# A graph layer on one core: self-edges taken out of the edge stream and added once per node block, packed rows stored end to end, one unit in 75 fetched row by row by SyncE

## The chip, the cores and the metric

The kernel runs on one core of one Trainium2 chip. The metric is the device time of one execution in microseconds, lower is better; the profile is one further execution of the same program with the hardware profiler on.

## The reference

There are 50,000 nodes with 160 numbers each (64 scalars `s`, then 32 vectors of 3) and 1,650,000 edges: 800,000 random pairs in both directions and one self-edge per node. The edges are sorted by their destination, so a node has 33 of them on average, one of which starts at the node itself. Every edge carries 4 numbers `sh`, and its message is bilinear in the source's row and these four:

```python
ss, vv = s[src], v[src];  e0, e1 = sh[:, 0:1], sh[:, 1:4]
dot  = einsum('eui,ei->eu', vv, e1)
out0 = C0 * (ss * e0 @ W1 + dot * INV3 @ W2)
p3 = (ss @ W3)[:, :, None] * e1[:, None, :] * INV3
p4 = einsum('eui,uw->ewi', vv * e0[:, :, None], W4) * INV3
p5 = einsum('eui,uw->ewi', cross(vv, e1[:, None, :]), W5) * INV6
m  = concat([out0, (C1 * (p3 + p4 + p5)).reshape(-1, 96)], axis=1)
m_agg = segment_sum(m, dst, num_segments=n)
h  = concat([m_agg[:, :64] @ Ws * LIN_S, (m_agg's vectors @ Wv) * LIN_V], axis=1)
x  = layernorm(x + (x + relu(h)))
```

All of it is linear in the source's row up to the relu. So for each node one may first sum, over its edges, the source's row times each of the four edge numbers (4 x 160 sums per node), and multiply that by one combined matrix of 640 x 160 afterwards. For a self-edge the source's row is the node's own, so its message needs no gathered row at all.

## The kernel before

*Units, groups, pairs, chunks, blocks.* 128 edges are a unit; 6 units (`G`) are a group of 768 edges, whose destinations lie in a window of 32 nodes (`W`); 2 groups are a pair, the step of the main loop (L637); 4 groups are a chunk of 128 window rows (`QG`); 20 groups, so 10 pairs, are a super group (`SG`), the amount that one load of edges brings. There are 1,050 pairs and 525 chunks. Output nodes are taken in 391 blocks of 128 (the last is shorter).

*One pair.* `gather` (L288) has GpSimd issue one indirect DMA per unit (L292), which brings the 128 source rows of 640 bytes into `xg`, on 6 buffers. `spread` (L297) has VectorE build, from each edge's place in the window (`rel`) and its four numbers (`pk`), a matrix `ha` of 128 edges x 128 columns (4 numbers x 32 window nodes) for each of 12 units (L301, L304), one pair ahead. `group_sums` (L329) has TensorE add up `ha` transposed times `xg`, 6 products per group (L334), into `ps` (128 x 160 per group, two groups a buffer). `ps` is then moved to `A` on 4 buffers, as the next paragraphs say.

*After a chunk.* At fixed numbers of pairs later (`after_pair`, L591, L662 to L669) the chunk is transposed (`turn`, L459), multiplied by the combined weights (`apply_weights`, L476, giving `hp`), and, once the last chunk that touches a node block is there, `nodes` loads the block's rows `xt` and builds one-hot matrices of the window rows' nodes (L493), `block` sums the rows `hp` of three chunks or so into nodes (L512), and the norm and the store of `out` follow over three more pairs.

*Loading edges.* `load` (L235) brings one super group's sources, destinations and numbers a super group ahead, `cast` makes floats of them, and `place` (L267) transposes them, so that each edge of a unit has a partition, and writes the gather indices `si` (L277) and `rel`. The destination of every group's first edge is read once at the start, out of DRAM into DRAM by three DMAs (L559, 2,020 numbers for the packed part) and back, broadcast to all partitions (L561), as `baseB`.

*Packing.* The first 60 groups (`NH`) are taken as they are. Each later group is made from a row of 786 edges (`L`), of which up to 18 (`K`) self-edges are taken out so that 768 remain. `pack` (L354) does this for 120 rows (`RP`), a row on each partition, 17 times in all: it reads the rows (`pri`, `pra`), marks self-edges and counts them (L390 to L398), collects the four numbers of each self-edge by window node into `mine` (L415 to L423, L419 most of all), moves the remaining edges down in 5 shifts of 1, 2, 4, 8, 16 places (L431 to L448), and stores 120 groups of 768 with three DMAs (L454, L455) into DRAM, from where `load` takes them. `pack` is a generator; the main loop advances it evenly over the 60 pairs until its rows are needed (L654 to L661), the first one over the 20 pairs or so that the head gives.

*The taken self-edges.* For each packed pair `own` (L311) loads the rows of x of both windows, repeated 4 times, into `xo` (one DMA per group, L324, at an address that is read from a table into a register, ten at a time, L318). When the pair's sums are done, VectorE moves `ps` to `A` and adds `xo` times the collected numbers `taken` (L343); for the head groups ScalarE copies (L339).

*Who issues what.* All these DMAs stand on SyncE's one queue (`dq`, L231), the gathers on GpSimd's, and seven loads of weights and three more on ScalarE's. `HELP` (L63) is empty: `fetch` (L537), which would load some units row by row from SyncE or ScalarE, one DMA per row at an address from a register, issues nothing. The order on each engine is that in which the program text emits instructions, as changed by the scheduler of the build; the buffers of the pools and semaphores do the rest. After the main loop a second pass over the edges stands in the program, with a loop count of zero unless a check on the data (L688) fails; both kernels have it alike.

Here is how one pair's gathers stand to the helped units, of which there are none in this kernel:

```python
for j in range(n - len(others)):
    nc.gpsimd.indirect_dma_start(out=xg[:, j, :], ..., in_=x, ...)
return [xg[:, j, :] for j in range(n - len(others))] + others
```

Of the kernel before, what the change touches and what calls it, by code (L numbers as in the profile page):

```python
# [25 lines left out]

# [17 lines left out]
P = 128  # L45
MUL0, MUL1 = 64, 32
D = MUL0 + 3 * MUL1
NK = 4
# [14 lines left out]
HELP = {}  # L63
HEAD = 60
RP = 120

# [3 lines left out]
def plan(n_nodes, n_edges):  # L70

    nblk = 125
    assert n_nodes % nblk == 0
    nb = n_nodes // nblk
    again = 9

    per_unit = P * n_nodes / n_edges
    group = max(g for g in range(1, 17)
                if g == 1 or (g + 0.2) * per_unit + 1 + 5 * math.sqrt(g * per_unit * per_unit / P) <= W)

    out = 0
    while out + 1 <= per_unit * group * (1 + 0.03) - 5 * math.sqrt(group * per_unit * per_unit / P + 1 / 6):
        out += 1
    row = group * P + out
    head = min(HEAD, math.ceil(n_edges / (group * P)))
    packed = max(0, (n_edges - head * group * P) // row // SG * SG) if out else 0
    rest = max(0, n_edges - head * group * P - packed * row)
    ngroups = head + packed + math.ceil(rest / (group * P))
    padded = QG * math.ceil(ngroups / QG)
    end = (head + padded - head - packed) * group * P + packed * row  # L90
    units = P * math.ceil(max(math.ceil(n_edges / P) + again - 1, math.ceil(end / P)) / P)
    return nblk, nb, again, group, units, ngroups, row, head, packed
# [3 lines left out]
def tile_gnn_resnorm(ctx: ExitStack, tc: tile.TileContext, x, src, dst, attr, W1, W2, W3, W4, W5, Ws, Wv, out, n_edges):  # L96
    nc = tc.nc
    N = x.shape[0]
    NBLK, NB, GA, G, NU, NG, L, NH, NPK = plan(N, n_edges)
    NCH = math.ceil(NG / QG)  # L100
    NGP = NCH * QG
    K = L - G * P

    def start(g):

        packed = min(max(g - NH, 0), NPK)
        return (g - packed) * G * P + packed * L

# [88 lines left out]
    def near(c):  # L197
        return start(c * QG) * N / n_edges

    step = QG * max(G * P, L) * N / n_edges  # L200
    off = 6 * math.sqrt(n_edges) / 2 * N / n_edges + W
# [10 lines left out]
    with tc.tile_pool(name="once", bufs=1) as once, tc.tile_pool(name="raw", bufs=2) as rawp, \  # L212
            tc.tile_pool(name="idx", bufs=2) as idxp, tc.tile_pool(name="rows", bufs=6) as rowp, \
            tc.tile_pool(name="far", bufs=3) as farp, tc.tile_pool(name="own", bufs=5) as ownp, \
            tc.tile_pool(name="pack", bufs=1) as packp, tc.tile_pool(name="self", bufs=2) as selfp, \
            tc.tile_pool(name="ops", bufs=3) as op, tc.tile_pool(name="sums", bufs=4) as sump, \
# [3 lines left out]
            tc.tile_pool(name="psM", bufs=2, space=PSUM) as psM:  # L220

        extremes = once.tile([P, 2, NSC], F32, name="extremes")
        baseB = once.tile([P, NGP], F32, name="baseB")
        rowid = once.tile([P, NCH], F32, name="rowid")
        bank = psC.tile([P, 3, P], F32, name="bank")
# [3 lines left out]

        own_eng = ET.Activation if ET.SP in HELP else ET.SP  # L230
        dq = nc.scalar if ET.SP in HELP else nc.sync  # L231
# [3 lines left out]
        def load(s):  # L235

            n = (min(NG, (s + 1) * SG) - s * SG) * G
            g0 = s * SG
            ra = rawp.tile([P, P, NK], F32, name="ra")
            if NH <= g0 < NH + NPK:  # L240
                sd, ad = stored[(g0 - NH) // RP]
                e = slice((g0 - NH) % RP * G * P, ((g0 - NH) % RP * G + n) * P)
                rf = rawp.tile([P, 2, P], F32, name="rf")
                for i in range(2):
                    dq.dma_start(rf[:n, i, :], sd[i:i + 1, e].rearrange("o (u p) -> (o u) p", p=P))
                dq.dma_start(ra[:n].rearrange("u p k -> u (p k)"), ad[e].rearrange("(u p) k -> u (p k)", p=P))
                return s, n, None, rf, ra
            e = slice(start(g0), start(g0) + n * P)
            ri = rawp.tile([P, 2, P], I32, name="ri")
            dq.dma_start(ri[:n, 0, :], src1[e].rearrange("(u p) o -> u (p o)", p=P))  # L250
            dq.dma_start(ri[:n, 1, :], dst1[e].rearrange("(u p) o -> u (p o)", p=P))
            dq.dma_start(ra[:n].rearrange("u p k -> u (p k)"), attr[e].rearrange("(u p) k -> u (p k)", p=P))
            return s, n, ri, None, ra

        def cast(loaded):
            s, n, ri, rf, ra = loaded
            if rf is None:
                rf = rawp.tile([P, 2, P], F32, name="rf")
                nc.scalar.copy(rf[:n], ri[:n])
            if HELP:  # L260

                ro = rawp.tile([P, P], I32, name="ro")
                nc.scalar.mul(ro[:n], rf[:n, 0, :], 4.0 * D)
                offsets[s] = ro
            return s, n, rf, ra

        def place(cast_):  # L267

            s, n, rf, ra = cast_
            pi = bank[:, 1:3, :]  # L270
            for i in range(2):
                nc.tensor.transpose(pi[:, i, :n], rf[:n, i, :], ident[:n, :n])
            pk = psK.tile([P, NK, P], F32, name="pk")
            for k in range(NK):
                nc.tensor.transpose(pk[:, k, :n], ra[:n, :, k], ident[:n, :n])
            si = idxp.tile([P, P], I32, name="si")
            nc.vector.tensor_copy(si[:, :n], pi[:, 0, :n])  # L277
# [4 lines left out]
                float(N - 1), baseB[:, s * SG:s * SG + n // G].unsqueeze(2).to_broadcast([P, n // G, G]),  # L282
# [26 lines left out]
        OWN = 5  # L309

        def own(p):  # L311

            s, g, ng = pairs[p]
            if not NH <= g < NH + NPK:
                return
            if p % OWN == 0:
                g1 = min(g + OWN * PG, NH + NPK)
                _, at = nc.values_load_multi_w_load_instructions(  # L318
                    baseO[0:1, g:g1], engines=[own_eng], min_val=0, max_val=(N - W) * 4 * D,
                    skip_runtime_bounds_check_because="an offset of a row of x")  # L320
                places.update(enumerate(at, g))
            xo = ownp.tile([P, PG, D], F32, name="xo")
            for i in range(ng):
                dq.dma_start(xo[:, i, :].bitcast(U8),  # L324
                             xbytes[ds(places.pop(g + i), W * 4 * D)].rearrange("(w f) -> w f", w=W).unsqueeze(0)
                             .to_broadcast([NK, W, 4 * D]))
            owns[p] = xo

        def group_sums(p, rows, ha):  # L329
# [7 lines left out]
            xo = owns.pop(p, None)  # L337
            if xo is None:
                evict(A[:, :ng], ps[:, :ng])  # L339
            else:  # L340
                for i in range(ng):
                    r = g0 - NH + i
                    nc.vector.scalar_tensor_tensor(A[:, i], xo[:, i], taken[r // RP][:, r % RP:r % RP + 1], ps[:, i],  # L343
                                                   op0=ALU.mult, op1=ALU.add)
            return A, ng

        owns, stored, taken, places = {}, {}, {}, {}
        halves = ((0, L // 2), (L // 2, L))

        degree = n_edges / N  # L350
        late = 6 * math.sqrt(L) + 2 * degree
        early = -6 * math.sqrt(L)

        def pack(c):  # L354

            r0 = c * RP
            n = min(RP, NPK - r0)
            e0 = start(NH + r0)
            e = slice(e0, e0 + n * L)
            prs = packp.tile([P, 2, L], F32, name="prs")  # L360
            pri = prs.bitcast(I32)
            pra = packp.tile([P, L, NK], F32, name="pra")
            pb = packp.tile([P, 1], I32, name="pb")
# [502 lines left out]
```

## Time and profile before

| | |
|---|---|
| runs | 15846.22, 15847.3, 15848.97 us; median 15847.3 |
| the profiled execution's own time | 15876.85 us |
| its span | 15875.1 us |
| TensorE's granted clock, mean | 0.669 |
| indirect gathers (L292) | 12,594 |
| products of a unit (L334) | 25,188 records, two for each unit |
| self-edge additions (L343) | 2,020, 682.1 us of VectorE |
| DMAs of `xo` (L324) | 2,020 |
| collecting self-edges' numbers (L419) | 2,856, 1492.2 us of VectorE |
| bytes moved | 1386.00 MB, 87 GB/s over the span |

The profile page gives, for one execution, the busy time of each engine and its share of the span (PE is TensorE's products, PEld its loads of the stationary matrix, DVE VectorE, ACT ScalarE, POOL GpSimd), then groups of instructions by program line with their mean duration, the idle time of their engine ahead of them, and what ended that idle time. Times are in us unless marked ns. Issuing a DMA doesn't count as busy; the DMA queues have a view of their own, in which an issue of SyncE stands under `SPq` with the smallest, the middle and the largest duration and the first and last start. In the view of waits a line is: engine, tile, line, what ended the wait, and then total us, number, longest.

### The profile page before, as it was taken

The page shows a single profiled execution, that of the slowest core. Times are in us where ns is not written, and L with a number is a line of the kernel's source. Part 1 is how long each engine was busy: PE and PEld are TensorE (multiplying, and loading weights), DVE is VectorE, ACT ScalarE, POOL GpSimd, SP SyncE. Part 2 cuts the span into 40 slices and gives each one's busy share as a digit, 9 for nine tenths or more (in the row PEclk, how much of TensorE's full clock was granted, in tenths as well). Part 3 has the DMA queues.
Part 4 walks back from the last instruction along what each step waited for, and adds up shares of the span by engine and source line. Part 5 has one row for each costly group of instructions (what it writes and reads, how often), then busy time and mean ns, then how long its engine had stood idle before and what let it go on. Part 6 is the DMA issues. An engine that isn't in the chain of part 4 may idle for free. (4 is left out here: it accounts for less than half of the span.)

```text
span 15875.1 us, 127140 instructions
## 1 busy us (share of the span) xinstructions
PE 12184.3 (77%) x43039; PEld 8889.9 (56%) x43040; DVE 6147.6 (39%) x14632; ACT 909.3 (6%) x2081; POOL 11939.1 (75%) x12606
## 2 busy tenths in 40 slices
PE   7677777777777777777777777777777777777777
PEld 5455555555555555555555555555555555555555
DVE  4543344443434343443434343433434343432222
ACT  0000000000000000000000000000000000000000
POOL 7777777777777777777777777777777777777776
PEclk6666666666666666666666666666666666666666
DMA  3333333333333333333333333333333333333332
GB/s 80 90 87 91 83 96 82 95 84 94 83 95 83 90 88 82 95 83 93 84 95 83 95 83 94 84 87 90 84 94 84 95 83 94 83 84 88 83 82 70
DMA packets 1045582, 1386.00 MB, mean 87 GB/s; under 512 B 233195, under 2 KB 818447, under 8 KB 1040753
## 3 DMA queue, kind: packets, MB, share of 16 engines
q0 software_dynamic: 604512, 1032.51, 27.0%
q1 hardware_dynamic: 439801, 344.75, 8.0%
q8 instruction: 338, 5.54, 0.2%
q14 instruction: 323, 2.65, 0.1%
q10 hardware_dynamic: 608, 0.55, 0.0%
HBM read 1307.42 MB, written 69.49 MB: 87 GB/s over the span
## 5 line engine op out<-in xcount | busy, mean ns | idle before, releaser
L292 POOL DMA_INDIRECT xg<-in_x,si x12594 | 11936.8, 948 | 3903.6 <-issue 3657.3
L334 PE MATMUL ps<-xg,ha 128*128 128x160 f32 x25188 | 8819.2, 457 | 3579.1 <-DMA xg<-in_x,si 3535.7
L334 PEld LDWEIGHTS ps<-xg,ha 128*128 128x128 f32 x25188 | 5613.2, 274 | 6208.0 <-DMA xg<-in_x,si 5628.7
L343 DVE SCALAR_TENSOR_TENSOR A<-xo,taken,ps 128x160 f32<-128x160 f32 x2020 | 682.1, 377 | 7006.9 <-PE ps L334 7003.6
L304 DVE TENSOR_TENSOR ha<-hot,pk 128x1536 f32<-128x1536 f32 x1050 | 1828.5, 1742 | 205.3 <-PE ps L334 205.3
L482 PE MATMUL phc<-BWb,at 32*128 32x160 f32 x4200 | 1610.1, 486 | 0.0
L419 DVE SCALAR_TENSOR_TENSOR waste<-marks,pra 120x236 bf16<-120x236 f32 (+45 forms) x2856 | 1492.2, 522 | 44.5
L512 PE MATMUL phb<-hp,hot 128*128 128x160 f32 x4538 | 1325.8, 395 | 0.3 <-DVE hot L502 0.2
L468 PE MATMUL pt<-ident,A 128*128 128x128 f32 (+1 forms) x4198 | 1292.2, 391 | 3.2 <-DVE A L343 0.9
L482 PEld LDWEIGHTS phc<-BWb,at 32*128 32x128 f32 x4200 | 919.3, 272 | 552.6 <-issue 552.6
L482 PE MATMUL phc<-BWa,at 128*128 128x160 f32 x4200 | 1149.4, 372 | 0.0
L512 PEld LDWEIGHTS phb<-hp,hot 128*128 128x128 f32 x4538 | 1082.1, 273 | 4.0 <-ACT at L471 3.5
L482 PEld LDWEIGHTS phc<-BWa,at 128*128 128x128 f32 x4200 | 919.5, 252 | 0.5 <-ACT at L471 0.2
L177 DVE SCALAR_TENSOR_TENSOR y<-phb,xt 128x160 f32<-128x160 f32 x391 | 125.8, 322 | 1969.8 <-PE phb L512 1969.1
L471 ACT COPY at<-pt 128x512 f32<-128x512 f32 (+1 forms) x1050 | 579.8, 579 | 4464.9 <-PE pt L468 4456.2
L468 PEld LDWEIGHTS pt<-ident,A 128*128 128x128 f32 (+1 forms) x4198 | 729.6, 176 | 87.6 <-DVE A L343 16.6
L301 DVE TENSOR_TENSOR hot<-bank,rel 128x384 f32<-128x384 f32 x1050 | 572.5, 546 | 2.4
L486 ACT COPY hp<-phc 128x160 f32<-128x160 f32 x525 | 153.6, 293 | 6019.0 <-PE phc L482 5982.1
L502 DVE TENSOR_TENSOR hot<-bank,rr 128x768 f32<-128x768 f32 (+2 forms) x391 | 357.9, 915 | 0.0
L186 ACT ACTIVATE rstd<-mv,eps_t 128x1 f32<-128x1 f32 x391 | 115.3, 295 | 3938.7 <-DVE mv L181 3902.5
L446 DVE COPY_PREDICATED pra<-marks,pra 120x1572 f32<-120x1572 int32 (+6 forms) x170 | 323.1, 1900 | 0.0
L419 DVE DVE_READ_ACCUMULATOR waste<-marks,pra 120x1 f32 (+1 forms) x2856 | 233.4, 82 | 0.0
(105 smaller groups left out, 1826.1 us busy)
## 6 DMA issues: line engine op xcount, KB each, us to landing
xg<-in_x,si POOLq DMA_INDIRECT x12594
xo<-in_x SPq DMA_DIRECT2D x2020, 80.0 KB
xt<-in_x SPq DMA_DIRECT2D x390, 80.0 KB
out<-o SPq DMA_DIRECT2D x390, 80.0 KB
ra<-ad SPq DMA_DIRECT2D x101, 240.0 KB
pra<-in_attr SPq DMA_DIRECT2D x16, 1475.6 KB
ad<-pra SPq DMA_DIRECT2D x16, 1440.0 KB
rf<-sd SPq DMA_DIRECT2D x202, 60.0 KB
```

Of the source, the lines that this page charges most:

```text
L292: nc.gpsimd.indirect_dma_start(out=xg[:, j, :], out_offset=None, in_=x, in_offset=bass.IndirectOffsetOnAxis(ap=placed[0][:, u + j:u + j + ...
L301: nc.vector.tensor_tensor(hot[:, :n], slotsP[:, 0:W].unsqueeze(1).to_broadcast([P, n, W]), rel[:, u:u + n].unsqueeze(2).to_broadcast([P, n ...
L304: nc.vector.tensor_tensor(ha[:, :n], hot[:, :n].unsqueeze(2).to_broadcast([P, n, NK, W]), pk[:, :, u:u + n].rearrange("p k u -> p u k").un ...
L334: nc.tensor.matmul(ps[:, j // G, :], ha[:, j].rearrange("p k w -> p (k w)"), xr, start=j % G == 0, stop=j % G == G - 1)
L343: nc.vector.scalar_tensor_tensor(A[:, i], xo[:, i], taken[r // RP][:, r % RP:r % RP + 1], ps[:, i], op0=ALU.mult, op1=ALU.add)
L419: nc.vector.scalar_tensor_tensor(waste[:n, w0:w1], m[:, w0 - a:w1 - a], float(w + 1), pra[:n, w0:w1, k], op0=ALU.is_equal, op1=ALU.mult, a ...
L446: nc.vector.copy_predicated(pra[:n, a:e], mi[:, r].unsqueeze(2).to_broadcast([n, e - a, NK]), pra[:n, a + d:e + d])
L468: nc.tensor.transpose(pt[:f1 - f0, g, :], A[:, i, f0:f1], ident)
L471: evict(at[:, :, :ng].rearrange("f k g w -> f g k w"), pt[:f1 - f0, :ng].rearrange("f g (k w) -> f g k w", w=W))
L482: nc.tensor.matmul(ph[:ng * W], at[:, k, :ng].rearrange("f g w -> f (g w)"), bw[:, k, :], start=i == 0, stop=i == 2 * NK - 1)
L502: nc.vector.tensor_tensor(hot2[:, :len(cs)], slotsP.unsqueeze(1).to_broadcast([P, len(cs), P]), rr[:, :len(cs)].unsqueeze(2).to_broadcast( ...
L512: nc.tensor.matmul(ph[:nb], hot2[:r, i, :nb], hp[:r], start=i == 0, stop=i == len(cs) - 1)
```

## The change

*Self-edges leave altogether.* `K` is gone; a row is now 790 edges (`L`), and up to 31 (`KM`) self-edges of a row are taken, that is, all. A row then leaves as many edges as it has that aren't self-edges, about 766, and the rows are stored one after another, each at the place where the one before ended, in one stream `edges` of 24 bytes per edge (source, destination and four numbers, all float). Groups are cut from this stream as 768 edges each, independent of the rows. There are 2,033 rows, still 17 packings of 120, but 2,086 groups, so 1,043 pairs and 12,516 units.

*Where a row goes.* A new `row_table` reads the destination of each row's first edge, 2,033 single numbers 790 apart, with one DMA into one partition (`ti`), bounds each, and works out each row's byte offset in the stream and its node's offset in `selves` (some fifteen VectorE operations on one partition, and an iota).

*Storing.* The store of a packing is 24 steps: 12 rounds (`RS`) for the rows' tails (places 32 and up), then 12 for their heads, so that what a row's tail writes too much is overwritten by the next row's head. A round reads ten stream offsets and ten node offsets into SyncE's registers and issues ten DMAs into `edges` and ten into `selves`, where the four numbers of each self-edge stand by node. All rounds of all packings: 8,128 DMAs instead of 51.

*Adding self-messages.* `own`, the loads of `xo` and the additions at L343 are gone: ScalarE copies `ps` to `A` for every pair. In their place `nodes` also loads the block's four self-edge numbers per node (`sa`, one DMA), and a new `own` of a block, three pairs after its last chunk, transposes `xt` (two transposes, ScalarE copies each), multiplies by the combined weights (four products of 320 columns), and weighs and sums the four parts with four VectorE operations into `t`; `block` adds `t` to the sums.

*Loading.* `load` takes a super group from the stream with one DMA (`r6`) instead of three. `place` works out the groups' first nodes from the loaded edges itself (one product with a matrix of ones, and a few VectorE operations), so that `base_d` and its DMAs are gone; `si` is held within 0 and N - 1.

*Fetching.* `HELP` is `{ET.SP: 75}`: of every 75 units one is brought by `fetch`, in four batches of 32 rows spread over the pairs ahead of its use, each batch one load of 32 offsets into registers and 32 DMAs of 640 bytes. In the built program these are 166 units, 21,248 DMAs and 664 loads of registers, all on SyncE, and 12,350 gathers remain on GpSimd. `dq` is now SyncE in any case (it was ScalarE when SyncE fetched).

*Spread and buffers.* The steps of a packing are a list of 102, dealt out over the pairs until `due`, one packing after another (due after pairs 19, 69, 129, 189 and so on, 60 apart). `xg` has 5 buffers instead of 6, `A` and `at` 3 instead of 4; the pool of `xo` is gone; `weights` and the table use a pool that is given back before the packing's begins. In the emitted text `place` of the first super group comes before the table and the weights.

```diff
-HELP = {}
+HELP = {ET.SP: 75}
...
-            tc.tile_pool(name="idx", bufs=2) as idxp, tc.tile_pool(name="rows", bufs=6) as rowp, \
-            tc.tile_pool(name="far", bufs=3) as farp, tc.tile_pool(name="own", bufs=5) as ownp, \
-            tc.tile_pool(name="pack", bufs=1) as packp, tc.tile_pool(name="self", bufs=2) as selfp, \
-            tc.tile_pool(name="ops", bufs=3) as op, tc.tile_pool(name="sums", bufs=4) as sump, \
+            tc.tile_pool(name="idx", bufs=2) as idxp, tc.tile_pool(name="rows", bufs=5) as rowp, \
+            tc.tile_pool(name="far", bufs=3) as farp, \
+            tc.tile_pool(name="ops", bufs=3) as op, tc.tile_pool(name="sums", bufs=3) as sump, \
...
-        dq = nc.scalar if ET.SP in HELP else nc.sync
+        dq = nc.sync
...
+                r6 = rawp.tile([P, P, 2 + NK], F32, name="r6")
+                dq.dma_start(r6[:n].rearrange("u p c -> u (p c)"),
+                             edges[0, p0 * (2 + NK):(p0 + n * P) * (2 + NK)].rearrange("(u q) -> u q", u=n))
...
-                for i in range(ng):
-                    r = g0 - NH + i
-                    nc.vector.scalar_tensor_tensor(A[:, i], xo[:, i], taken[r // RP][:, r % RP:r % RP + 1], ps[:, i],
-                                                   op0=ALU.mult, op1=ALU.add)
+            evict(A[:, :ng], ps[:, :ng])
...
+            with nc.allow_non_contiguous_dma(reason="one number of each row"):
+                dq.dma_start(ti[:, :NR], dst[EH:EH + NR * L].rearrange("(o r e) -> o r e", o=1, e=L)[:, :, 0])
...
-            for i in range(2):
-                dq.dma_start(sd[i:i + 1].rearrange("o (r e) -> (o r) e", e=G * P), prs[:n, i, :G * P])
-            dq.dma_start(ad.rearrange("(r e) k -> r e k", e=G * P), pra[:n, :G * P])
+            def store(head, j):
+                m = len(range(j, n, RS))
...
+                _, at = nc.values_load_multi_w_load_instructions(row_at[0:1, i0:i0 + m], engines=[ET.SP], ...)
+                _, node = nc.values_load_multi_w_load_instructions(node_at[0:1, i0:i0 + m], engines=[ET.SP], ...)
+                for i in range(m):
...
+                    e = slice(0, W) if head else slice(W, L)
+                    put(edge_bytes, v, e, C, T["rows"][p:p + 1, e, :])
...
+                        e = slice(0, W // 2) if head else slice(W // 2, W)
+                        put(self_bytes, v, e, NK, T["mine"][p:p + 1, 0, e, :])
...
+            for head in (False, True):
+                steps += [partial(store, head, j) for j in range(RS)]
...
+            sa = np_.tile([P, NK], F32, name="sa")
+            dq.dma_start(sa[:nb], selves[0, row.start * NK:row.stop * NK].rearrange("(n k) -> n k", k=NK))
...
+        def own(b, xt, sa, hot2):
+            nb, row = rows_of(b)
+            pt = psM.tile([P, 2, P], F32, name="ptx", tag="misc")
+            xT = np_.tile([P, 2, P], F32, name="xT")
+            for i, (f0, f1) in enumerate(((0, P), (P, D))):
+                nc.tensor.transpose(pt[:f1 - f0, i, :nb], xt[:nb, f0:f1], ident[:nb, :nb])
+                evict(xT[:f1 - f0, i, :nb], pt[:f1 - f0, i, :nb])
+            t = np_.tile([P, D], F32, name="t")
+            for h in range(NK // 2):
+                y = psM.tile([P, 2, D], F32, name="yx", tag="misc")
+                ks = slice(2 * h, 2 * h + 2)
+                nc.tensor.matmul(y[:nb], xT[:, 0, :nb], BWa[:, ks, :], start=True, stop=False)
+                nc.tensor.matmul(y[:nb], xT[:D - P, 1, :nb], BWb[:, ks, :], start=False, stop=True)
+                for i in range(2):
...
+                        nc.vector.scalar_tensor_tensor(t[:nb], y[:nb, i], sa[:nb, k:k + 1], t[:nb],
+                                                       op0=ALU.mult, op1=ALU.add)
...
+            nc.vector.tensor_tensor(ph[:nb], ph[:nb], t[:nb], op=ALU.add)
...
+            if packs:
+                todo = math.ceil(len(packs[0]) * min(1, (p + 1 - began) / max(1, due[0] - began)))
+                for step in packs[0][done:todo]:
+                    if step:
+                        step()
...
+                    after_pair(p + 3, do_own, b)
```

The function that fetches, unchanged, is in both kernels; with `HELP` set it is what SyncE runs for each batch:

```python
_, at = nc.values_load_multi_w_load_instructions(
    offsets[s][u:u + 1, i * nr:(i + 1) * nr], engines=[eng], ...)
for j, v in enumerate(at):
    r = i * nr + j
    queues[eng].dma_start(xr[r:r + 1, :].bitcast(U8), xbytes[ds(v, 4 * D)]...)
```

## The prediction

> **What bounds the kernel now.** I read the busy shares first, then the costliest groups, then the waits, then the order of time.
>
> ```profile
> PE 12184.3 (77%) x43039; PEld 8889.9 (56%) x43040; DVE 6147.6 (39%) x14632; ACT 909.3 (6%) x2081; POOL 11939.1 (75%) x12606
> L292 POOL DMA_INDIRECT xg<-in_x,si x12594 | 11936.8, 948 | 3903.6 <-issue 3657.3
> ```
> ```profile
> POOL xg L292 <- issue: 3657.3, 11997, 0.4
> PE ps L334 <- DMA xg<-in_x,si: 3535.7, 5300, 7.2
> ```
> ```profile
> 5000.30 0.95 POOL L292 DMA_INDIRECT xg<-in_x,si  x1 [0.30 <-issue]
> 5001.56 0.94 POOL L292 DMA_INDIRECT xg<-in_x,si  x1 [0.30 <-issue]
> ```
>
> PE and POOL look equally busy, but PE waits 3535.7 us for gathered rows, while POOL waits for nobody: its idle time is 0.30 us of "issue" after each 0.95 us gather. The starts are 1.2525 us apart (median over the run), and 12,594 x 1.2525 = 15,774 of the 15,875 us span. The rest is 18.7 us ahead of the first gather, 50 us in slower gaps, and 33 us after the last. So the number of gathers is the time, as long as every buffer comes free for POOL. SP sets nothing today, but these are its prices:
>
> ```profile
> L324 SPq DMA_DIRECT2D xo<-in_x x2020: 539/562/1667, 39.2 to 15629.0; - x184
> L498 SPq DMA_DIRECT2D xt<-in_x x391: 328/359/495, 20.8 to 15835.6; - x196
> L615 SPq DMA_DIRECT2D out<-o x391: 332/342/481, 165.0 to 15863.7; - x196
> L318 SPq TENSOR_LOAD <-baseO x202: 1138/2244/2619, 37.9 to 15566.0; - x101
> ```
>
> These are min/median/max in ns. A DMA costs SP about a third of a microsecond whatever its size; the one with an address from a register, 562 ns (its view has three dimensions too). Ten numbers into registers cost 1.1 to 2.6 us.
>
> **What the Trainium skill says.** "Perfetto Trace Analysis", section "DMA Instruction — HWDGE (DVE, Sync)": the profiled time of such a DMA is the sequencer's own, descriptor generation included, and only at its end is the sequencer free. The trace agrees: two xo DMAs stand as 1.20 to 1.24 us in a row. "DMA: Bandwidth & Descriptors", section "Why a DMA increments its semaphore by 16 and not by 1": a DMA is spread over the largest number up to 16 that divides both sides' slowest dimension. No run here shows that number directly; it matters for the startup. "Runtime: NRT & Kernel Launch", section "Instruction fetch mechanics", gives about 200 ns a register for a load; the trace has 114 to 262 ns each for ten.
>
> **The change, part by part.**
>
> *Fewer gathers.* The built program has 12,350: 78 units fewer because no self-edge is left, and 166 fetched by SP. 244 x 1.2525 = 306 us less.
>
> *Startup.* The new row table reads 2,033 single numbers with one DMA into one partition. Its relative before was this:
>
> ```profile
> 2.15 7.32 SPq L559 DMA_DIRECT2D base_d<-in_dst  x3
> 18.00 0.37 SPq L561 DMA_DIRECT2D baseB<-base_d  x1
> 18.74 1.11 POOL L292 DMA_INDIRECT xg<-in_x,si  x1 [15.82 <-DVE si L277]
> ```
>
> The last of the three begins at 3.9 and SP sees them landed at 18.0: 14 us for 2,020 numbers, which by the skill's rule go over 10 engines, 202 each, or 70 ns a number. 2,033 = 19 x 107 has no divisor up to 16 but 1, so all go over one engine: 2,033 x 70 ns = 142 us (an estimate). In DVE's order of the changed program the first operation on this table (L361) stands ahead of the one that writes `si`, and every gather waits for `si`. First gather near 150 instead of 19: +130 us. Bounds: 0 if it is spread, 150 at most. I take 130.
>
> *SP's new work.* One fetched unit: 128 DMAs and four loads of 32 numbers. For a row's DMA I take 0.38 us: 0.33 (lowest of `out` and `xt`) and 0.05 to the next. Bounds 0.30 (lowest of any static DMA, 0.28, with little gap) and 0.67 (562 ns, its 38 ns MOVE, and gaps). A load of 32: 2.2 (like a slow ten) to 8.4 (3.2 x 2.6); I take 3.6, i.e. 3.2 x 1.14. Unit: 128 x 0.38 + 4 x 3.6 = 63 us, in the 94 us that 75 units take. Beside it the rows of each packing are no longer stored by three DMAs but by 24 rounds of 20, each with two loads of ten and ten register additions of 0.04: 20 x 0.38 + 0.4 + 2 x 1.8 = 11.6 us, 278 us for one packing.
>
> *Where this collides.* A packing is laid out over 60 pairs in 102 equal steps, the stores being the last 24, so 14.1 pairs. A pair takes 12 x 74/75 x 1.2525 = 14.8 us: 209 us. In that stretch SP has 278 of stores, 14.1 x 12/75 = 2.26 units of 63 = 142, and 17 other DMAs, 7: together 427. SP ends 218 us behind. Over the whole 60 pairs (888 us) it has 605 + 278 + 34 = 917 us of work, so it is full on average too. Queued behind SP's stores, in its one order, are the fetched rows, `xt`, the block's self-sums and the next edges; PE waits for each, in order, and POOL then for PE to free `xg`. What absorbs it: SP's fetches stand about 3 to 4 pairs ahead of their use in the built order (45 to 60 us), and `xg` has 5 buffers, 4 of them ahead (60 us). I take 120 us; 80 to 150 is possible. So 218 - 120 = 98 us lost per packing, 16 times: +1,570 us. PE then catches up within the quieter 46 pairs.
>
> *The first packing* has only 20 pairs. In before it already came late:
>
> ```profile
> 487.44 0.39 PEld L272 LDWEIGHTS bank<-ident,rf 120*128 120x128 f32 x2 [65.52 <-DMA rf<-sd]
> 489.16 0.95 POOL L292 DMA_INDIRECT xg<-in_x,si  x1 [16.14 <-DVE si L277]
> ```
>
> Now its reads start after the table (about 165), DVE needs some 200 us (168 sums of 553 + 82 ns, 107 us, and the shifts and spreads between), and 278 of stores with five quarter fetches follow: stored near 730. POOL has used its 360 units at 150 + 356 x 1.25 = 596. Stall 139 instead of 16: +123 us.
>
> *The rest.* The 2,020 additions of xo (377 ns, DVE) leave; A's copies go to ACT (1,004 more of 0.43 us, on an engine 6% busy). The self-sums per block cost DVE 5 operations of about 0.33 us and PE two transposes (0.31) and four products of 320 columns (twice the 2,759 us / 4,200 of L482, 1.3 us each), 5.9 us, 2,300 us in all: PE goes from 12,184 to about 14,400 busy, under POOL's pace, so I count nothing. If that cover is thin it costs as in the third rival. ACT's two small copies of xT put PE in wait some 1 us a block, hidden too. ACT issues no data DMA after the weights either way.
>
> *Sum* against the profiled execution's 15,877: - 306 + 130 + 123 + 1,570 = 17,394. The median of the runs is 30 below that execution, so 17,360.
>
> **Rivals.** *SP keeps up (faster).* At 0.30 us a DMA, 2.2 for a load of 32 and 1.2 for one of ten, the stretch holds 24 x 8.8 = 211, 2.26 x 47 = 107 and 5: 323, which is 114 behind and within the 120. That decides: below about 0.30 us a DMA nothing is lost per packing. Then 15,847 - 306 + 130 + 45 (first packing) = 15,716; 15,560 if the table is spread and the first packing hides. For it: the smallest static DMAs are at 0.28 to 0.29. Against: `xt` and `out` sit at 0.34 to 0.36, and dynamic ones at 0.56. *SP is full everywhere (slower still).* At 0.45 us and 8.4 a unit is 91 us, a round 13.9, and 60 pairs cost 875 + 334 + 35 = 1,244: 17.2 such cycles, 21,400. For it: the loads' price by the skill; against: no static DMA's median is above 0.43. *PE becomes the bound.* 14,400 busy of 15,570 leaves 8%, and its bursts end in POOL waiting for `xg`; with the startup's 130 and some 200 lost, 15,870, no change. For it, 77% before; against, the granted clock rises where PE is busy (0.76 at 500:600 against 0.50 at 450:500). That the change doesn't do what it says is excluded by the built program's counts.
>
> **How the numbers follow.** SP behind by bursts: 0.70, 17,360, its own range 16,500 to 18,700. SP keeps up: 0.19 (0.17 faster, 0.02 about equal). SP full everywhere: 0.05. PE bound: 0.06 (0.02 equal, 0.04 slower). The measurement tells some 0.2% (32 us) from no change. Faster 0.17, same 0.04, slower 0.79. The range has to reach the second case: 15,650 to 18,700 leaves out part of it and the third.
>
> **What would show it.** Right: in the second half of each 60-pair cycle PE's waits name the DMA of `xr0` or `xt`, POOL's gaps grow from "issue" to PE or `si`, SP's DMAs follow each other without a pause there; the first gather near 150. Wrong: row DMAs well under 0.30 us, POOL at 1.25 us throughout, first gather near 19.

## The result, and the profile after

The changed kernel takes 17,719.35 us (median of four runs, 17,712.38 to 17,724.04) against 15,847.53 (15,846.22 to 15,848.97): 1.118 times as long, 95% interval 1.116 to 1.120. It is slower by 1,872 us, where 1,513 had been forecast.

The page of the changed kernel, busy shares and the group of the gathers:

```profile
PE 10659.9 (60%) x47011; PEld 7822.1 (44%) x47012; DVE 6717.7 (38%) x15105; ACT 1589.0 (9%) x3978; POOL 11687.7 (66%) x12364
...
L302 POOL DMA_INDIRECT xg<-in_x,si x12350 | 11683.4, 946 | 5971.7 <-issue 3593.2
```

The 244 gathers fewer are there, but POOL's idle time has grown from 3903.6 to 5971.7 us, and "issue" is no longer nearly all of it. From the waits (us in total, times, longest):

```profile
POOL xg L302 <- issue: 3593.2, 11787, 1.1
PE ptx L607 <- DMA xt<-in_x: 2829.4, 84, 224.0
...
POOL xg L302 <- PE ps L324: 2297.3, 408, 185.4
...
DVE mine L416 <- DMA selves<-mine: 729.7, 14, 81.4
...
PE ps L324 <- DMA xr<-in_x: 312.8, 21, 50.0
```

POOL now waits 2,297 us for TensorE to free `xg`. TensorE waits for the block's x rows (`xt`, 2,829 us), and only 313 us for the fetched rows (`xr`). Both are SyncE's. One packing's cycle in stretches of 100 us (busy us of PE, PEld, DVE, ACT and POOL, with numbers of instructions, then the granted clock, the DMA share and GB/s):

```profile
1100.00:1200.00 100.00, 74.18 (x285) 51.29 (x285) 25.43 (x50) 8.32 (x22) 75.62 (x81) 0.67 0.30 76
1200.00:1300.00 100.00, 74.48 (x313) 53.01 (x311) 29.88 (x60) 10.64 (x28) 75.61 (x81) 0.69 0.32 83
1300.00:1400.00 100.00, 18.15 (x69) 13.14 (x70) 8.47 (x10) 2.12 (x6) 66.58 (x71) 0.53 0.26 67
1400.00:1500.00 100.00, 31.72 (x169) 26.18 (x168) 13.45 (x26) 4.50 (x13) 45.37 (x48) 0.64 0.17 43
1500.00:1600.00 100.00, 46.26 (x225) 35.37 (x226) 50.46 (x122) 14.62 (x25) 44.44 (x47) 0.63 0.31 73
1600.00:1700.00 100.00, 53.32 (x319) 44.78 (x317) 94.52 (x325) 9.61 (x27) 64.43 (x69) 0.76 0.27 66
1700.00:1800.00 100.00, 52.93 (x319) 46.41 (x320) 75.71 (x119) 10.08 (x26) 56.62 (x60) 0.74 0.23 58
1800.00:1900.00 100.00, 80.63 (x358) 58.45 (x357) 34.36 (x64) 11.60 (x31) 75.60 (x80) 0.75 0.29 73
```

The stores of this packing run from 1139.1 to 1525.5. There are two different losses: from 1300 to 1525 TensorE and VectorE have nothing to do (PE 18 of 100 us); from 1600 to 1800 VectorE has too much (94.5 of 100). What the first one is, the order of time shows:

```profile
1355.81 0.37 SPq L734 DMA_DIRECT2D out<-o  x1
...
1358.48 10.79 SPq L667 DMA_DIRECT2D xr<-in_x  x32
...
1389.80 0.38 SPq L589 DMA_DIRECT2D xt<-in_x  x1
...
1391.68 0.48 PE L607 MATMUL ptx<-ident,xt 128*128 128x128 f32 x1 [69.94 <-DMA xt<-in_x]
```

Between the batch of fetched rows and `xt` stand 40 stores, the first at 1371.76. SyncE issues `xt` at 1389.80, and TensorE, which had stood still for 69.94 us, goes on 1.9 us later. SyncE is without a pause, and a load of 80 KB that takes 2 us is late because of its place in the order.

Worked out from the starts of all gathers (every gap over 1.3 us, less 1.2525), the changed kernel loses 2,199 us: 278 at the first packing, 119 per packing at the other 16 (72 while the stores are issued, 47 in the 400 us after), and 20 elsewhere. The account then closes: 15,875 - 306 (244 gathers) + 5 (first gather) + 2,199 - 52 (the slower gaps of before) + 25 (longer end) - 28 (the other gaps are 1.2501 instead of 1.2524 on average) = 17,718, and the span is 17,719.1.

### The profile page after: what moved, and what is told of

Read it like the earlier page. It is cut to its first block, busy times and chain, and to the rows that moved or that the text cites. A ratio compares the mean times of both kernels' runs of the same rounds, so it can differ in the third digit from the quotient of the medians.

```text
span 17719.1 us, 198822 instructions
## 1 busy us (share of the span) xinstructions
PE 10659.9 (60%) x47011; PEld 7822.1 (44%) x47012; DVE 6717.7 (38%) x15105; ACT 1589.0 (9%) x3978; POOL 11687.7 (66%) x12364
## 4 chain that ended last, share of the span: by engine, by line
SPq 24%; POOL 22%; issue 16%; DVE 16%; PE 13%; DMA 7%; another core or an unknown queue 0%; ACT 0%; DVEq 0%; ACTq 0%; POOLq 0%
POOL xg L302 22%; SPq L540 9%; DVE pra L465 7%; SPq L667 6%; PE ps L324 4%; DMA xg<-in_x,si 4%; SPq L519 3%; SPq L522 3%; PE phb L630 2%; DVE ha L314 2%; DVE prow L504 2%; PE pt L559 2%; PE phc L573 2%; DMA edges<-prow 2%; SPq L662 2%
## 5 line engine op out<-in xcount | busy, mean ns | idle before, releaser
L302 POOL DMA_INDIRECT xg<-in_x,si x12350 | 11683.4, 946 | 5971.7 <-issue 3593.2
L324 PE MATMUL ps<-xg,ha 128*128 128x160 f32 x24700 | 5320.4, 360 | 1563.9 <-DMA xg<-in_x,si 1465.3
L324 PEld LDWEIGHTS ps<-xg,ha 128*128 128x128 f32 x24700 | 4045.2, 218 | 2761.0 <-DMA xg<-in_x,si 2450.3
L314 DVE TENSOR_TENSOR ha<-hot,pk 128x1536 f32<-128x1536 f32 x1043 | 1823.6, 1751 | 4215.5 <-PE ps L324 4214.9
L607 PE MATMUL ptx<-ident,xt 128*128 128x128 f32 (+2 forms) x782 | 289.9, 371 | 3095.8 <-DMA xt<-in_x 2829.4
L559 PE MATMUL pt<-ident,A 128*128 128x128 f32 (+1 forms) x4172 | 924.4, 375 | 1547.4 <-DVE t L620 1381.9
L607 PEld LDWEIGHTS ptx<-ident,xt 128*128 128x128 f32 (+2 forms) x782 | 114.3, 146 | 3242.4 <-DMA xt<-in_x 1544.8
L465 DVE SCALAR_TENSOR_TENSOR pra<-marks,prow 120x236 bf16<-120x236 f32 (+40 forms) x2924 | 1508.4, 516 | 77.5
L559 PEld LDWEIGHTS pt<-ident,A 128*128 128x128 f32 (+1 forms) x4172 | 549.7, 156 | 1990.8 <-issue 1802.3
L614 PE MATMUL yx<-BWb,xT 32*128 32x320 f32 x1564 | 967.8, 713 | 75.3 <-ACT xT L608 75.3
L613 PE MATMUL yx<-BWa,xT 128*128 128x320 f32 x1564 | 916.8, 683 | 0.4 <-ACT xT L608 0.3
L573 PE MATMUL phc<-BWb,at 32*128 32x160 f32 x4176 | 708.7, 309 | 0.0
L573 PE MATMUL phc<-BWa,at 128*128 128x160 f32 x4176 | 695.2, 312 | 0.2 <-ACT at L562 0.2
L614 PEld LDWEIGHTS yx<-BWb,xT 32*128 32x128 f32 x1564 | 339.6, 269 | 649.8 <-ACT xT L608 327.3
L573 PEld LDWEIGHTS phc<-BWb,at 32*128 32x128 f32 x4176 | 582.1, 186 | 90.8 <-issue 90.4
```

The source lines that it names most:

```text
L302: nc.gpsimd.indirect_dma_start(out=xg[:, j, :], out_offset=None, in_=x, in_offset=bass.IndirectOffsetOnAxis(ap=placed[0][:, u + j:u + j + ...
L314: nc.vector.tensor_tensor(ha[:, :n], hot[:, :n].unsqueeze(2).to_broadcast([P, n, NK, W]), pk[:, :, u:u + n].rearrange("p k u -> p u k").un ...
L324: nc.tensor.matmul(ps[:, j // G, :], ha[:, j].rearrange("p k w -> p (k w)"), xr, start=j % G == 0, stop=j % G == G - 1)
L465: nc.vector.scalar_tensor_tensor(T["waste"][:n, w0:w1], T["marks"][:n, w0 - a:w1 - a], float(w + 1), T["rows"][:n, w0:w1, 2 + k], op0=ALU. ...
L559: nc.tensor.transpose(pt[:f1 - f0, g, :], A[:, i, f0:f1], ident)
L573: nc.tensor.matmul(ph[:ng * W], at[:, k, :ng].rearrange("f g w -> f (g w)"), bw[:, k, :], start=i == 0, stop=i == 2 * NK - 1)
```

## The experiments

Each was timed side by side with the kernel before. That took 15,887 us beside x4, x6, x7 and x8, and 15,847 to 15,849 beside the others, so below stands the difference from it; the changed kernel's is +1,872.

**x1, nothing fetched.**

```diff
-HELP = {ET.SP: 75}
+HELP = {}
```

> The changed kernel with nothing fetched row by row: HELP is empty, all 12,516 units are gathered. The built order of VectorE's packing steps also becomes even by this (172 collecting operations over 27 pairs instead of over 8). Theory A (SyncE is too full while a packing is stored, because the fetches stand in the same stretch): SyncE then has 24 x 10.8 = 260 us of stores and 5 us of other DMAs in a stretch of 209 us, 56 behind, which the buffers hide; 166 gathers more cost 208; the first packing still comes some 150 late: 12,516 x 1.2525 + 24 + 58 + 150 = 15,910 us, GpSimd without gaps from 900 us on. Theory B (the stores alone are too much, since the block's x rows are asked for only one pair ahead): half of the 120 us per packing stays, 16,870 us. Theory C (TensorE's new self-sums are the bound): no loss goes away, 17,900 us.

Measured: 16,064.15 us, +216. Its waits:

```profile
PEld pk L285 <- DMA r<-edges: 325.9, 2, 322.5
...
POOL xg L302 <- DVE si L287: 301.2, 2, 281.4
...
POOL xg L302 <- PE ps L324: 212.9, 619, 12.7
...
PE ptx L607 <- DMA xt<-in_x: 128.1, 5, 66.8
```

From 1,500 us on no packing costs anything; the 272 to 280 us of a packing's stores (291 once) are hidden. Of 340 us lost, 281 are the first packing (one wait of POOL for `si`, which waits for the first edges from the stream) and 24 the second. So theory C falls: the self-sums cost no time here. Nor do the stores alone, which speaks against B; what costs is stores and fetches in the same pairs. But two other things changed with it. VectorE's order became even, which the next run separates. And SyncE issues the x rows 102 us ahead of their use here (median outside the stores), against 58 in the changed kernel, so this run alone doesn't exclude that the longer lead hid the stores. x10 below does: its lead is 64 us, and its stores cost next to nothing.

**x5, VectorE in the text's order.** In the changed kernel's trace a packing's 172 collecting operations (L465) stand within 7 to 9 pairs, with up to 81 us of work between two of the operations that build `ha` (L314). In this run they stand over 22 to 26 pairs: each operation of a packing step is held behind what the text emits before it on VectorE (an order, not a wait):

```diff
                     if step:
+                        at = len(nc.cur_bb.bb.instructions)
                         step()
+                        for ins in list(nc.cur_bb.bb.instructions[at:]):
+                            if ins.engine == ET.DVE:
+                                pin(ins)
```

> The changed kernel with VectorE's packing operations held in the order in which the program text deals them out; the built order of the changed kernel has nearly all of a packing's some 200 us of VectorE in 9 pairs, this one over 37. Stores and fetches are as they were. Theory A (two losses per packing: 73 us while SyncE stores, 45 us afterwards, when VectorE's bunched work holds up the matrices that TensorE waits for): the second goes, 17,719 - 16 x 45 = 17,000 us. Rival (what is lost afterwards is SyncE's catching up): 17,700 us.

Measured: 17,143.96 us, +1,296. The stretches after the stores of the same packing (these end at 1,499):

```profile
1500.00:1600.00 100.00, 47.38 (x247) 36.70 (x245) 55.40 (x130) 13.53 (x24) 60.86 (x65) 0.71 0.35 88
1600.00:1700.00 100.00, 86.10 (x456) 70.75 (x456) 66.14 (x198) 15.80 (x40) 75.61 (x81) 0.80 0.31 83
1700.00:1800.00 100.00, 73.16 (x283) 49.50 (x282) 46.49 (x129) 7.49 (x21) 75.61 (x81) 0.67 0.26 71
```

VectorE has 66 instead of 94.5 us in the stretch, PE 86 instead of 53, and POOL is back at 75.6, its full pace. The loss after the stores falls from 47 to 9 us per packing (5 without the last), the one within them stays (75). VectorE's wait for the stores to leave `mine` (L416) is as long as before, 722.9 us, so that wait isn't the cause of the second loss; in this kernel the bunching is. It isn't enough by itself, though. In x2 below, which has the fetching alone, a packing's collecting operations stand within 5 to 10 pairs too, with up to 65 us between two `ha` after the first packing, and nothing is lost. What makes the changed kernel sensitive to it (5 instead of 6 buffers of `xg`, the self-sums' operations in the same order of VectorE, or longer bunches) no run took apart.

**x4, the stores dealt over some 30 pairs.**

```diff
-                todo = math.ceil(len(packs[0]) * min(1, (p + 1 - began) / max(1, due[0] - began)))
+                part = min(1, (p + 1 - began) / max(1, due[0] - began))
+                work = len(packs[0]) - 2 * RS - 1
+                todo = math.ceil(work * min(1, 2 * part) + (2 * RS + 1) * max(0, 2 * part - 1))
```

> The changed kernel with a packing's 24 store steps dealt over some 30 pairs instead of 14 (the other 78 steps take the first 30); VectorE's built order stays bunched as in the changed kernel. Theory A (73 us per packing are lost because stores and fetches overfill SyncE in 14 pairs; 45 more because VectorE's work is bunched): in 30 pairs, 444 us, SyncE has 260 of stores, 240 of fetches and 20 others, 76 behind, which the buffers hide: 17,719 - 16 x 73 = 16,550 us. Rival 1 (the bunching costs only because TensorE is late already): 15,830 us. Rival 2 (SyncE is full over the whole cycle): 17,500 us or more.

Measured: 16,415.48 us, +528, so 1,344 less than the changed kernel (1,170 expected). The loss while storing is gone (0 to 0.1 us per packing from the third on); after the stores 37 us remain, with VectorE's order as bunched as it was. So each loss stands largely without the other, and rival 1, with its 15,830 us, misses.

**x6, both.** The two diffs above.

> Both: stores dealt over some 30 pairs, and VectorE's packing operations held in the text's order. Theory A: both losses go, only the first packing's 278 us stay: 17,144 - 16 x 77 = 15,910 us. Rival 2 (SyncE is full over the whole cycle): 17,000 us.

Measured: 16,136.03 us, +249; expected was +63. Nothing is lost while storing; 272 us at the first packing, 13 after each of the others and 98 at the end of the last full one stay. The built order of this one is less even than that of x5 (from the second packing on up to 59 collecting operations in one pair, 27 in x5), since its 78 steps have half the pairs.

**x7, the x rows asked for earlier.** On top of x5, `xt` and `sa` are loaded one chunk and two pairs earlier, into buffers of their own:

```diff
+        def ask(b):
+            nb, row = rows_of(b)
+            xt = nxp.tile([P, D], F32, name="xt")
+            dq.dma_start(xt[:nb], x[row, :])
...
+                for b in after[min(c + AHEAD, NCH - 1)] if c + AHEAD < NCH else []:
+                    ask(b)
```

> The changed kernel with VectorE's packing operations held in the text's order (17,144 us with that alone), and the block's x rows and self-edge numbers asked for one chunk and two pairs earlier, still on SyncE; no other change. Theory A (SyncE ends 165 us behind; the x rows with their short lead are met first, the fetched rows next, at 120): 45 instead of 77 us per packing, 16,630 us, TensorE's waits name the fetched rows. Theory B (the short lead is all of it): 15,910 us. Theory C (whatever is asked for is as late): 17,140 us.

Measured: 16,831.36 us, +944, 351 less than x5 (A: 514, B: 1,234, C: 0). From `xt`'s issue to its use there were 60 to 77 us in the upper four tenths in the changed kernel, 85 to 118 here. The loss while storing falls from 75 to 50 us. But TensorE's waits still name `xt` (1,916.6 us), not the fetched rows: A is nearest in size, but what it said of the waits is not there. That the lead is part of the loss is shown; that the fetched rows would be late next is not.

**x3, the x rows on ScalarE's queue.**

```diff
-            dq.dma_start(xt[:nb], x[row, :])
+            nc.scalar.dma_start(xt[:nb], x[row, :])
...
-            dq.dma_start(sa[:nb], selves[0, row.start * NK:row.stop * NK].rearrange("(n k) -> n k", k=NK))
+            nc.scalar.dma_start(sa[:nb], selves[0, row.start * NK:row.stop * NK].rearrange("(n k) -> n k", k=NK))
```

> The changed kernel with the block's two loads (its rows of x and its self-edge numbers) on ScalarE's queue; fetches and stores stay on SyncE. Theory A (SyncE is behind by 165 us at a packing's end, and the block's x rows, one pair ahead of their use, are only what TensorE meets first; the fetched rows are next, 120 us of cover): 45 instead of 73 us are lost while a packing is stored, what is lost afterwards stays: 17,719 - 16 x 28 = 17,270 us, TensorE's waits name the fetched rows. Theory B (the short lead of the x rows is the whole loss of the stretch): 17,719 - 16 x 73 = 16,550 us. Theory C (everything on SyncE is equally late): 17,700 us.

Measured: 20,021.78 us, +4,173. All three theories miss. What SyncE waits for in this run:

```profile
SPq L667 <- DMA sa<-selves: 2622.1, 254, 114.9
SPq L667 <- DMA xt<-in_x: 2378.8, 259, 56.0
SPq L540 <- DMA sa<-selves: 793.1, 78, 32.2
SPq L540 <- DMA xt<-in_x: 464.8, 82, 17.0
```

SyncE's own row DMAs now wait 6,259 us for DMAs that ScalarE has issued, or has yet to issue, and which have no data in common with them. In the built program the DMAs of both queues take turns on the same eight semaphores, and each waits until the one before it on its semaphore has landed. On one queue that is soon over; but ScalarE issues behind its evictions, which wait for TensorE. That the semaphores couple the queues is read from the waits and the built program; no run took it apart. For the question at hand the run decides nothing.

**x8, both and a longer head.** x6 with `HEAD = 100`, so that the first packing has 40 pairs.

> Stores spread and VectorE in the text's order, and 100 instead of 60 groups taken as they are at the start, so that the first packing has 40 pairs. Theory: the first packing's 278 us go, some 7 gathered units for the self-edges of 40 more groups come: 15,910 - 278 + 9 = 15,640 us, below the kernel before and level with the kernel before with fetching. Rival (the first packing is late by its own chain of work, not for lack of pairs): 15,900 us.

Measured: 15,911.59 us, +24; -207 was expected. The first packing loses 127 instead of 272 us, the second still 63, the rest some 10 each: 349 in all. The lack of pairs was half of it.

**x11, nothing fetched, and the longer head.**

> The changed kernel with nothing fetched and 100 instead of 60 groups taken as they are at the start. Theory: of the 340 us that GpSimd lost in the run without fetching, 305 were the first two packings' lateness; with 40 pairs for the first they go, and 12,522 x 1.2525 + 24 + 55 = 15,765 us remain: self-edges' leaving is worth some 80 us when its stores stand alone on SyncE. Rival (the first packing is bound by its own chain of reads, VectorE's work and stores, whatever the pairs): 16,050 us.

Measured: 15,854.16 us, +7, ratio 1.0004 (0.9996 to 1.0013). 95 us are still lost at the first packing and 129 in all, more than the 72 gathers saved (90 us). So this half of the change, with a longer head and nothing fetched, brings nothing. What it would bring without the 129 us no run shows.

**x2, only the fetching, in the kernel before.**

```diff
-HELP = {}
+HELP = {ET.SP: 75}
...
-        own_eng = ET.Activation if ET.SP in HELP else ET.SP
-        dq = nc.scalar if ET.SP in HELP else nc.sync
+        own_eng = ET.SP
+        dq = nc.sync
```

> The kernel before with the row-by-row fetching of one unit in 75 by SyncE and nothing else of the change. Theory A (fetching pays as long as SyncE isn't full): a unit takes SyncE 4 x 2.2 + 128 x 0.323 = 50 us, 75 units last 94 us, and the other DMAs of that time some 10 us; 168 gathers fewer x 1.2525 = 210 us, so 15,640 us. Rival (21,500 small DMAs disturb the gathers, or the rows of x of the self-edges come late behind them): no gain, 15,850 us or more, with GpSimd's pace above 1.2525 us or its gaps put down to TensorE.

Measured: 15,642.25 us, -206, ratio 0.9871 (0.9854 to 0.9887): all that 167 gathers are worth. Its waits:

```profile
POOL xg L292 <- issue: 3606.1, 11832, 0.3
POOL xg L292 <- PE ps L334: 140.4, 442, 5.4
```

GpSimd's slower gaps cost 59 us in the whole run, 52 in the kernel before, and its other starts stay 1.25 us apart: the small DMAs don't disturb the gathers, and the rival falls. This is the lowest time of the study.

**x9 and x12, fetching more.** x2 with `HELP = {ET.SP: 50}` and `HELP = {ET.SP: 40}`.

> The kernel before, with one unit in 50 fetched by SyncE. A unit costs SyncE 50 us, the other DMAs about 7 us, in the 61 us that 49 gathers take: 93% full. Theory A (nothing is lost as long as SyncE's work fits): 12,343 gathers, 251 fewer, 15,848 - 251 x 1.2525 = 15,534 us. Rival (SyncE must have slack well above that, since its DMAs come in bursts): above 15,642 us.

> The same with one unit in 40, past the point. Theory A (SyncE then sets the time): 314 units of 50 us and about 5.5 us of other DMAs each in 49 us: 314 x 55.5 = 17,430 us, SyncE without pauses, TensorE waiting for fetched rows. Rival (row DMAs get cheaper, or SyncE isn't what sets it): 15,848 - 314 x 1.2525 = 15,455 us.

Measured: x9 16,447.58 us, +600, and x12 19,407.06 us, +3,560. x9 missed because the prices were too low: a batch takes 13.2 us with its load and gaps, a unit 52.7 (not 50). In x2 SyncE pauses for 4,368 us (pauses over 1 us between its instructions), so its other work is 15,640 - 4,368 - 167 x 52.7 = 2,470 us, which is 9.8 for each of 251 units (not 7). That makes 62.5 us of work in 61 us: it was full. With these prices, and its own pauses (729 and 518), SyncE takes 251 x 52.7 + 2,470 + 729 = 16,430 in x9 and 314 x 52.7 + 2,470 + 518 = 19,540 in x12, for spans of 16,446.2 and 19,403.7. Work and pauses fill any span, so what this shows is that the prices held and that SyncE hardly paused (4% and 3% of the span). In x12 the waits name its loads:

```profile
PE ps L334 <- DMA xr<-in_x: 4959.8, 219, 41.9
DVE y L177 <- DMA xt<-in_x: 4611.7, 323, 40.4
```

In x2 SyncE works 11,270 of 15,640 us, 72%, and nothing is lost.

**x10, fetching only where nothing is stored.** x5 with `HEAD = 100`, and a unit is skipped if one of its batches falls into the pairs in which a packing is stored:

```diff
+                if any(storing(p) for p in at):
+                    first += period
+                    continue
```

> The changed kernel with VectorE in the text's order, 100 groups as they are at the start, and no fetching in the pairs in which a packing is stored (106 units fetched instead of 166). Theory: stores and fetches never meet on SyncE, so neither costs anything: 12,416 x 1.2525 + 24 + 55 = 15,630 us. Rival (SyncE is still behind when fetching starts again, or the block's x rows are late behind the stores alone): 16,000 us or more.

Measured: 15,671.81 us, -176, ratio 0.9888 (0.9872 to 0.9905). Its waits:

```profile
POOL xg L302 <- issue: 3573.8, 11718, 3.0
...
PE ptx L607 <- DMA xt<-in_x: 189.0, 12, 47.5
POOL xg L302 <- PE ps L324: 171.7, 470, 23.4
```

81 us are lost in the whole run, 31 of them at the first packing and some 2 to 5 at each of the others. TensorE's wait for `xt` is 189 us in total instead of 2,829, though `xt` has about the short lead of the changed kernel: that lead matters only where the queue ahead of it is full. The buffers of `xg` and `A` are as few as in the changed kernel, so they cost little here.

## Why the prediction was right, and where its sum was off

The likeliest case, SyncE behind by bursts, is what happened; the time lies in its own range (16,500 to 18,700). By its steps:

- *Fewer gathers*, -306: as counted. (The 1.2525 us called a median is nearer the mean of the starts that aren't delayed, 1.2524; the median is 1.2530.)
- *Startup*, +130: measured +5. This is the term that failed outright. The lines:

```profile
3.36 0.76 SPq L358 DMA_DIRECT2D ti<-in_dst  x1
...
17.65 1.21 DVE L361 TENSOR_SCALAR node<-ti 1x2040 f32<-1x2040 int32 x1 [11.26 <-DMA ti<-in_dst]
...
23.59 0.28 DVE L287 TENSOR_SCALAR si<-bank 128x120 int32<-128x120 f32 x1
...
24.16 3.83 POOL L302 DMA_INDIRECT xg<-in_x,si  x1 [19.89 <-DVE si L287]
```

The order was as foreseen: L361 ahead of `si`, and VectorE waiting for the table. But the 2,033 numbers were there 14.3 us after the start of their DMA's issue, 7 ns each with everything else in it, not 142 us. I had read the 14 us of the kernel before as the time of 202 numbers on each of ten engines, 70 ns a number; but the issue of that DMA alone had taken 5.5 of them (the longest at L559), and a number is cheap. The rule on spreading, cited from the Trainium skill ("DMA: Bandwidth & Descriptors", "Why a DMA increments its semaphore by 16 and not by 1"), isn't contradicted: the DMA share of the stretch from 7 to 17 us is 0.10, one or two of 16 engines. What it does not give is a price per number, and I made one from the wrong row.
- *SyncE's new work.* A unit 63, measured 52.7; the durations behind it:

```profile
L667 SPq DMA_DIRECT2D xr<-in_x x21248: 227/228/3034, 19.4 to 17540.2; - x199
```
```profile
L662 SPq TENSOR_LOAD <-ro x664: 2042/2162/2890, 17.1 to 17527.9; - x166
```

From start to start a row takes 0.323 us (0.38 taken), a load of 32 numbers 2.16 (3.6 taken, from 3.2 times that of ten). The price isn't proportional to the count: the loads of ten take 1.77 and 1.84 us here (medians at L519 and L522), so some 180 ns a register. That is near the 200 ns that the Trainium skill's "Runtime: NRT & Kernel Launch", section "Instruction fetch mechanics", gives for TENSOR_LOAD "even for bulk" (of the runtime's own loads, from HBM; these are from a tile). A load of 32 takes 68 ns a register, and here the measurement decides. A packing's stores 278, measured 272 to 280 where no fetch stands between them (x1). Three readings behind these prices were wrong. The case of SyncE keeping up was to be told by a row's DMA under 0.30 us: the instruction lasts 0.228, but with its MOVE and the gaps the starts are 0.323 apart, and it is the step that counts. "Whatever its size" holds for whole rows of data (in the kernel before, DMAs of 57 to 1,476 KB at fixed addresses cost SyncE 0.32 to 0.50 us in the median), but not for single numbers: the three DMAs at L559 took 0.74, 0.96 and 5.52 us, so "no static DMA's median is above 0.43" was wrong too. And SyncE wasn't "full on average": its pauses over 1 us add up to 3,732 us in the changed kernel, so it has 13,990 us of work for the 15,570 that an undelayed run would take, 90%. It is overfull only where the stores are.
- *The collision*, 98 per packing. With the measured prices: 272 + 2.26 x 52.7 + 7 = 398 in 209 us, 189 behind, less 120 of cover: 69. Measured while storing: 72. So the step holds in its place and mechanism. That the size fits to 3 us is luck in part: the 120 was an estimate (80 to 150), no run measured it, and it was worked out for the fetched rows, while the x rows were late first, with a lead of their own. They had been listed as queued, not as first.
- *"PE then catches up within the quieter 46 pairs"*: wrong. VectorE's packing work was taken as even, as the text deals it out; in the built order it stands in 7 to 9 pairs, where the kernel before has it in 30 to 34, and that costs most of the 47 us after the stores (38 of them go in x5). 98 predicted, 119 measured: the price of SyncE was too high by about 29, and this term of 47 was missing; the two errors pull in opposite directions.
- *The first packing*, +123: measured 278. (The working gives 730 - 596 = 134 us of stall, 118 more than before, where 139 and 123 were written.) I let POOL run out of head edges; in truth TensorE stopped earlier, 224 us for an `xt` of the head behind the first stores. x1 shows that without fetches the delay is as long, there through the first edges.
- *The rest*, nothing: right. x1 runs without gaps from 1,500 us on with the self-sums in it. They take TensorE 2,175 us (L607, L613 and L614 in the changed kernel), near the 2,300 forecast. Yet 14,400 us busy was wrong: 10,660, and 12,332 in x1, where GpSimd keeps its pace. The other products did not keep their mean: a record at L324 is 360 ns (421 in x1) where it was 457 at L334, so the busy time before plus that of the new work was too much.
- *The signs.* Of those named for being right, TensorE's wait for `xt`, GpSimd's gaps put down to TensorE and SyncE without a pause while storing are there. The first gather at 24 us is a sign that had been named for being wrong.

The time was 359 us above the forecast. Startup (-125) and first packing (+155) nearly cancel; 16 x 21 = 336 us come from VectorE's bunched work, less what SyncE's price had been set too high.

## What to carry to other kernels

A queue has to be priced for the stretch in which its jobs meet, not as a mean: SyncE had time for the fetches (x2, 72% full, the whole gain) and for the stores (x1), and the kernel lost 72 us each time they fell into the same 14 pairs; keeping them apart, with VectorE in the text's order and a longer head (x10), gives nearly all of it back. What the queue falls behind costs nothing until it passes the lead of the first load that stands behind it. Read that lead and every engine's share of work per pair from the built order, not from the text: here switching on the fetching alone drew VectorE's packing work from some 32 pairs together into 5 to 10 (x2). And where a change joins two ideas, time each alone: here the fetching was worth 206 us, and the other half cost 216 as it was written (x1) and nothing with a longer head (x11).

## What the runs showed that was not expected

- Row-by-row DMAs at addresses from registers stand 0.323 us apart, less than the fixed-address loads `xt` and `out` (0.37 each, alone). With an addition for the address ahead of each second one (the tails' stores) it is 0.392 from start to start.
- 2,033 single numbers, 790 apart, are in one partition 14.3 us after the start of one DMA's issue.
- DMAs moved to a second queue made the first one wait 6,259 us for them (x3).
